# Nucleus search of step 2: three rounds that aim 6.5 values short, in place of four that aim 8 short

## The chip, the cores and the metric

The kernel runs on one core of a Trainium2 chip. The metric is the device time of one execution in microseconds (us), as a median of several runs. Engines are named as in the profile: PE (TensorE matmul), PEld (TensorE weight load), DVE (VectorE), ACT (ScalarE), POOL (GpSimd), SP (SyncE, here mostly the issuer of loads).

## The reference, cut to what matters

There are 2708 nodes with 512 features. Layer 0 is a graph attention layer. Layer 1 makes two steps (s = 0, 1; this document calls them step 1 and step 2, as the change does). Each step builds an attention matrix over all node pairs, keeps of each row only the nucleus (the largest values, until they hold 90% of the row's mass), and multiplies:

```python
def _adj_from_feats(Xa, W1, W2, W3):
    logits = (Xa @ W1) @ W2 @ (Xa @ W3).T
    idx = jnp.argsort(-logits, axis=1)
    vals = jnp.take_along_axis(logits, idx, axis=1)
    csum = jnp.cumsum(jax.nn.softmax(vals, axis=1), axis=1)
    k_i = jnp.sum(csum < 0.9, axis=1) + 1          # how many of each row are kept
    ...
    return jax.nn.softmax(masked, axis=1)          # the others are -inf

for s in range(2):
    A = _adj_from_feats(Xa, W1, W2, W3)
    Xf = Rf @ Xf
    Xb = Rb @ Xb
    Xa = A @ Xa
    Z = Z + (Xf @ U1[s] + Xb @ U2[s] + Xa @ U3[s])
Y = X + Z                                          # then a layer norm, and the residual
```

Rf and Rb are the row- and column-normalised adjacency.

## The kernel before, in words

**Tiles.** The 2708 rows are 22 tiles of 128 (the last has 20 rows). Attention works on pairs of tiles: 11 pairs, numbered 0 to 10. For one pair the work goes through these stages:

- `queries` loads the pair's queries, `products` (PE, line 570) makes the logits of both tiles against all 2708 keys, and ACT copies them to two SBUF tiles `p` (line 572). There are four buffers `p`, so two pairs' worth.
- the row maximum (`maxima`, DVE, line 597), then `exp`: ACT turns `p` into exponentials, POOL works out three first guesses of the threshold, ACT looks at the mass above each (`junk_a`, line 604, twelve passes over 2708 columns), and POOL adds these looks up (`masses`, line 629, tile `pts`).
- `Opened.ready` (line 691) and `bracket` (from line 697): DVE takes from the three looks the two points of each row that lie on either side of the wanted mass.
- `search`: in each round `point` (lines 718 to 726, nine tiny DVE instructions) picks a threshold between the two ends, `measure` (line 683, one DVE pass over 2708 columns for each tile of the pair, with an accumulator) finds the mass above it, and five tiny instructions (lines 768 to 773) move one of the ends. `AIM` says by how many values the search aims to stop short of the wanted mass, so that it ends just above the nucleus' last value. `ROUNDS` is the number of rounds in step 1 and step 2.
- `finish`: for each tile, the `NEXT` largest values below the threshold are taken, eight at a time (a masked copy into `keep[0]`, line 877, then MAX8, line 879). Among these the last value of the nucleus is found; `kept_ranked` (lines 817 to 820) writes the kept exponentials to `keep`, ordering equal values by `rank`. `NEXT` is 16 in step 2 before and after.
- `branch`: a code is loaded from SBUF and DVE branches on it (line 961). If a row of the pair did not find its last value among the 16, `short` sets the code and `bisect` runs for the pair: 27 halvings with two passes each, then two scans of each tile. If only the number of equal values does not come out, `ties` runs for a tile (lines 826 to 836, with a scan over 2708 columns, line 831).
- the reciprocal of the kept mass (`rden`, line 972) ends the pair's search. `attended` then transposes `keep` on PE (line 1146), ACT copies the transposes (line 1150), and PE multiplies them with the values (line 1168). There are two buffers `keep`, one pair's worth.

**Order.** The schedule of PE, ACT, DVE and SP is written out by hand. The loop over g runs from -1 to 10. In iteration g, PE first makes `products` of pair g + 2, then `attended` of pair g. Between its pieces are put, as `others`, the products with the adjacency matrix (line 1042, operands `hl` of 512 KB and `s_r` of 256 or 192 KB loaded by SP for every one, in 3 and 4 buffers) and with U1 and U2 (line 1062), shared out evenly over the pairs by `price`; and as `fills` the ACT steps of `exp` of pair g + 2. What is left of both comes in a loop at the iteration's end. Meanwhile DVE runs `search` of pair g + 1. In its rounds are put: before the second measurement and after the second round the two maxima of pair g + 2 (`early`'s first two functions); before the third measurement the layer norm statistics of the rows finished one iteration ago (line 153); and before the fourth measurement the rest of that norm (lines 1242 and 1243, tile `yo`). SP stores these rows (line 1244) at one fixed place of its in-order queue, in the middle of `attended`; loads that come later in the program wait behind that store.

The search's rounds read:

```python
        for it in range(ROUNDS[s]):
            o.point(s > 0 and it == 0)
            if it == 1:
                afterwards.extend(early())
            if afterwards:
                afterwards.pop(0)()
            o.measure()
            ...
            if it == 1:
                afterwards.pop(0)()
        for rest in afterwards:
            rest()
```

Of the kernel before, what the change touches and what calls it, by code (L numbers as in the profile page):

```python
# [42 lines left out]

CURVE = 0.4
CAP = 0.06
AIM = (4.0, 8.0)
ROUNDS = (2, 4)
NEXT = (8, 16)

TINY = 2.0 ** -80  # L50
# [4 lines left out]
def kernel(  # L55
# [591 lines left out]
    class Opened:  # L647
# [27 lines left out]
        def aim(self, dst, th):  # L675
            v, lg = nc.vector, self.lg
            v.scalar_tensor_tensor(dst, th, AIM[lg.s], lg.cap, op0=OP.mult, op1=OP.min)
            v.scalar_tensor_tensor(dst, lg.tot, 1.0 - P_NUC + CURVE, dst, op0=OP.mult, op1=OP.add)
# [58 lines left out]
    def search(lg, o, junk, early, late):  # L737
# [22 lines left out]
        afterwards = []  # L760
        for it in range(ROUNDS[s]):
            o.point(s > 0 and it == 0)
# [723 lines left out]
```

## Time and profile before

| what | us |
|---|---|
| median of 3 runs (3461.5 to 3477.28) | 3462.85 |
| the profiled execution's own time | 3462.71 |
| its span, first to last instruction | 3460.9 |
| PE busy | 3183.6 (92%) |
| DVE busy | 2573.5 (74%) |
| ACT busy | 1502.3 (43%) |
| POOL busy | 933.6 (27%) |

Times inside the profile are counted from the span's start. Step 1's pairs run from about 1000 to 2050, the first search of step 2 ends at 2292.9, its other ten searches end at 2396.7, 2513.9, 2634.6, 2740.8, 2844.1, 2951.4, 3073.8, 3180.1, 3302.1 and 3401.9 (line 972), and the rest is the last pair's product and norm. An "x" in a row counts instructions; "idle before" is the time that the engine stood still ahead of them, with what ended most of it. A PE that is shown busy need not be at its peak, since the ends of matmuls are modelled.

### The profile page before, as it was taken

To read this page: it belongs to the slowest core of one execution; us is meant where nothing else is said; L and a number is where in the kernel's file an instruction comes from. 1 tells how busy PE (TensorE), PEld (TensorE's weight loads), DVE (VectorE), ACT (ScalarE), POOL (GpSimd) and SP (SyncE) were. 2 spreads that over 40 slices of the span, in tenths; PEclk is the share of its full clock that TensorE was granted. 3 is DMA by queue.
4 is the path that set the end of the run, shared out by engine and by line. 5 is a ranking of instruction groups with operands and counts; after the bars stand their busy time and mean duration, and the time that the engine had idled before them with its cause. 6 is when DMAs were issued, how large, how long until landed. Compare 5 with 4: busy or idle time off the path is not lost. (4 is left out here: it accounts for less than half of the span.)

```text
span 3460.9 us, 44356 instructions
## 1 busy us (share of the span) xinstructions
PE 3183.6 (92%) x16033; PEld 1695.6 (49%) x16033; DVE 2573.5 (74%) x4485; ACT 1502.3 (43%) x2219; POOL 933.6 (27%) x1091
## 2 busy tenths in 40 slices
PE   7988899998888999999999998899988999998998
PEld 4543333332455446455564643555555555555553
DVE  4588899899857564463745634997999899898893
ACT  2333231111046766665657622346544564455510
POOL 4221743607221222122122312111321233122211
PEclk9998999999999999999999999999999999999999
DMA  4478554222386245254453534865544653556553
GB/s 135 153 240 271 188 176 146 85 93 87 114 291 222 92 143 206 67 187 165 140 181 122 199 124 141 281 220 189 188 137 139 207 200 125 175 182 220 182 178 123
DMA packets 240046, 580.65 MB, mean 168 GB/s; under 512 B 32863, under 2 KB 66107, under 8 KB 239657
## 3 DMA queue, kind: packets, MB, share of 16 engines
q1 hardware_dynamic: 217721, 503.38, 43.9%
q0 software_dynamic: 22064, 74.09, 5.6%
q8 instruction: 127, 2.08, 0.2%
q14 instruction: 134, 1.10, 0.1%
HBM read 471.68 MB, written 105.68 MB: 167 GB/s over the span
## 5 line engine op out<-in xcount | busy, mean ns | idle before, releaser
L1168 PE MATMUL a<-va,at 128*128 128x512 f32 (+2 forms) x1936 | 887.2, 598 | 4.7 <-ACT at L1150 4.6
L483 PE MATMUL po<-e,fw 128*32 128x384 f32 (+3 forms) x7392 | 675.7, 502 | 65.7 <-DVE e L477 38.7
L477 DVE SCALAR_TENSOR_TENSOR e<-r_b,kk,a_c 128x768 f32<-128x768 f32 (+3 forms) x704 | 659.7, 997 | 50.4 <-PE po L483 41.8
L604 ACT ACTIVATE junk_a<-p,nth 128x2708 uint8<-128x2708 f32 (+1 forms) x240 | 612.7, 2553 | 38.1 <-POOL nth L619 33.6
L1042 PE MATMUL q<-hl,s_r 128*128 128x512 f32 x1936 | 541.5, 426 | 70.8 <-DMA s_r<-s_d 49.8
L1168 PEld LDWEIGHTS a<-va,at 128*128 128x128 f32 (+2 forms) x1936 | 338.2, 186 | 373.8 <-issue 341.4
L1042 PEld LDWEIGHTS q<-hl,s_r 128*128 128x128 f32 x1936 | 365.1, 193 | 235.5 <-issue 67.2
L483 PEld LDWEIGHTS po<-e,fw 128*32 128x32 f32 (+1 forms) x7392 | 256.9, 112 | 449.7 <-issue 260.0
L1150 ACT COPY at<-t 128x512 f32<-128x512 f32 (+3 forms) x308 | 140.9, 478 | 652.4 <-PE t L1146 648.6
L683 DVE SCALAR_TENSOR_TENSOR junk<-p,th 128x2708 bf16<-128x2708 f32 (+1 forms) x132 | 407.3, 3086 | 3.0
L1062 PE MATMUL q<-u_k,v 128*128 128x512 f32 x704 | 316.9, 592 | 1.1 <-ACT v L1052 1.1
L1045 PE MATMUL q<-s_r,hl 128*128 128x512 f32 (+1 forms) x1056 | 279.7, 409 | 17.7 <-DMA s_r<-s_d 15.1
L1045 PEld LDWEIGHTS q<-s_r,hl 128*128 128x128 f32 x1056 | 193.2, 189 | 97.7 <-issue 49.9
L1062 PEld LDWEIGHTS q<-u_k,v 128*128 128x128 f32 x704 | 133.3, 190 | 158.9 <-issue 154.2
L570 PE MATMUL t<-keys,q_t 128*128 128x452 f32 x528 | 158.7, 424 | 52.4 <-ACT p L572 50.6
L572 ACT COPY p<-t 128x452 f32<-128x452 f32 (+2 forms) x264 | 131.5, 537 | 172.0 <-PE t L570 128.0
L879 DVE MAX8 vn<-keep 128x8 f32<-128x2708 f32 (+1 forms) x66 | 196.8, 2981 | 2.3
L597 DVE TENSOR_REDUCE nmx<-p 128x1 f32<-128x2708 f32 (+1 forms) x44 | 130.5, 2967 | 63.9 <-ACT p L572 63.9
L1215 PE MATMUL a<-u_k,v_t 128*128 128x512 f32 (+1 forms) x352 | 170.2, 624 | 4.7 <-ACT yo L1222 3.0
L155 POOL TENSOR_SCALAR ln_rs<-ln_mv 128x1 f32<-128x1 f32 x66 | 49.6, 752 | 412.8 <-DVE ln_mv L154 411.5
L1146 PEld LDWEIGHTS t<-ident,keep 128*128 128x128 f32 (+1 forms) x968 | 115.5, 139 | 77.5 <-issue 48.0
L1146 PE MATMUL t<-ident,keep 128*128 128x128 f32 (+1 forms) x968 | 146.0, 273 | 3.5 <-ACT p L572 2.8
(311 smaller groups left out, 3435.3 us busy)
## 6 DMA issues: line engine op xcount, KB each, us to landing
hl<-vhl_d SPq DMA_DIRECT2D x132, 512.0 KB
s_r<-s_d SPq DMA_DIRECT2D x264, 256.0 KB
hl<-fhl_d SPq DMA_DIRECT2D x132, 512.0 KB
hl<-bhl_d SPq DMA_DIRECT2D x132, 512.0 KB
u_k<-in_L_gnn_U_dram SPq DMA_DIRECT2D x184, 256.0 KB
arow<-in_adj_dram SPq DMA_DIRECT2D x42, 677.0 KB
s_d<-a_f SPq DMA_DIRECT2D x66, 384.0 KB
s_r<-s_d SPq DMA_DIRECT2D x132, 192.0 KB
```

The lines of the kernel that those rows point to most:

```text
L477: nc.vector.scalar_tensor_tensor(es[i][:pr, :cw], r_b[:pr, i, :cw], kk[:pr, t, grp[i]:grp[i] + 1], a_c[t][:pr, :cw], op0=OP.max, op1=OP.mult)
L483: nc.tensor.matmul(po[k][n][q * w:(q + 1) * w, :b - a], lhsT=of if d < DH else of.to_broadcast([pr, w]), rhs=es[i][:pr, a:b], start=(t == ...
L570: nc.tensor.matmul(pl[:, :c1 - c0], lhsT=q[:, i], rhs=self.keys[:, c0:c1], start=(i == 0), stop=(i == 1))
L604: nc.scalar.activation(junk[:pr], self.p[i][:pr], func, **kw)
L683: nc.vector.scalar_tensor_tensor(self.junk_b[:pr], p, th, p, op0=OP.is_ge, op1=OP.mult, accum_out=dst)
L879: v.max(vs, keep[0][:pr])
L1042: nc.tensor.matmul(half[j], lhsT=s_r[:, j * P:(j + 1) * P], rhs=hl[:, h], start=(c == 0 and h == 0), stop=(c == NT - 1 and h == 1))
L1045: nc.tensor.matmul(half[j][:, :w], lhsT=hl[:, h, j * P:(j + 1) * P], rhs=s_r[:, :w], start=(c == 0 and h == 0), stop=(c == NT - 1 and h == 1))
L1062: nc.tensor.matmul(half[j], lhsT=across_t[-1][k][:, j * P:(j + 1) * P], rhs=u_k, start=(start and k == 0), stop=(start and k == KD - 1))
L1146: nc.tensor.transpose(pt[:rows[c], j, :pr], keep[i][:pr, cols[c]], ident[:pr, :pr])
L1168: nc.tensor.matmul(pa[:pr], lhsT=at[:rows[c], j, :pr], rhs=va[:rows[c], c, :], start=(c == 0), stop=(c == NT - 1))
L1215: nc.tensor.matmul(pz[i][:rows[t]], lhsT=v_t[i][:, k, :rows[t]], rhs=u_k, start=(k == 0), stop=(k == KD - 1))
```

## The change

Two constants change. `AIM` and `ROUNDS` hold a value for step 1 and one for step 2; those of step 1 and `NEXT` stay. In step 2 every pair's search makes three rounds, and aims 6.5 values short of the wanted mass. The rest of the norm (lines 1242 and 1243) then follows the third round instead of standing between the fourth round's `point` and its measurement. On PE, ACT, POOL and SP the instructions and their order are the same, but for the place of the empty block joins of line 961 among them.

```diff
 CURVE = 0.4
 CAP = 0.06
-AIM = (4.0, 8.0)
-ROUNDS = (2, 4)
+AIM = (4.0, 6.5)
+ROUNDS = (2, 3)
 NEXT = (8, 16)
```

## The prediction

> **What bounds the kernel now.** First the page's busy shares: PE 92%, DVE 74% over the whole span. That is an average, so next the windows view, cut at the ends of step 2's searches (line 972). Columns: length, then busy us of PE, PEld, DVE, ACT, POOL, then the granted PE clock, DMA share, GB/s.
>
> ```profile
> 2513.80:2634.50 120.70, 106.67 (x360) 64.18 (x360) 111.34 (x189) 61.45 (x72) 26.32 (x22) 0.95 0.49 164
> 2740.70:2844.10 103.40, 95.85 (x321) 56.96 (x322) 94.25 (x180) 58.02 (x66) 29.53 (x22) 0.97 0.46 157
> 2951.40:3073.80 122.40, 112.23 (x372) 65.55 (x371) 110.60 (x189) 58.86 (x68) 26.39 (x24) 0.97 0.55 183
> 3180.10:3302.10 122.00, 111.55 (x373) 63.88 (x374) 108.52 (x189) 56.95 (x65) 22.39 (x21) 1.00 0.62 212
> ```
>
> A pair of step 2 takes 100 to 122 us, and both DVE and PE stand still for only some 10 us of it. DVE's 10 us are its own chain, not waits: some 5 us of it follow the branch of line 961 in nearly every pair. So two engines are close to full, and the question is which one sets the pace where. The waits of PE between 2292 and 3402 answer it; they come to about 90 us.
>
> ```profile
> L1042 PE MATMUL q<-hl,s_r 128*128 128x512 f32 x1584 | 449.8, 430 | 56.7 <-DMA s_r<-s_d 36.1 <-ACT xe L1086 20.0
> L570 PE MATMUL t<-keys,q_t 128*128 128x452 f32 x216 | 68.0, 443 | 29.0 <-ACT p L572 29.0
> ```
>
> PE waits mostly for loads and for ACT, hardly for DVE by name. But line 572 writes the buffers `p` that DVE's `finish` reads, so I looked in the timeline at what ACT waited for each time PE stood still at line 570, and at the one long load wait:
>
> ```profile
> 2405.65 6.58 PE L570 MATMUL t<-keys,q_t 128*128 128x452 f32 x17 [4.87 <-ACT p L572]
> 2513.88 0.97 ACT L572 COPY p<-t 128x452 f32<-128x452 f32 x2 [14.96 <-DVEq L961]
> 2514.47 7.51 PE L570 MATMUL t<-keys,q_t 128*128 128x452 f32 x20 [5.30 <-ACT p L572]
> 2634.67 0.97 ACT L572 COPY p<-t 128x452 f32<-128x452 f32 x2 [9.36 <-DVE keep L836]
> 2635.26 3.62 PE L570 MATMUL t<-keys,q_t 128*128 128x452 f32 x8 [9.22 <-ACT p L572]
> 2740.81 0.97 ACT L572 COPY p<-t 128x452 f32<-128x452 f32 x2 [17.51 <-DVEq L961]
> 2741.39 1.11 PE L570 MATMUL t<-keys,q_t 128*128 128x452 f32 x4 [2.07 <-ACT p L572]
> 3302.04 1.06 PE L1146 MATMUL t<-ident,keep 128*128 128x128 f32 x8 [0.62 <-DVEq L966]
> 3342.37 1.84 SPq L1244 DMA_DIRECT2D out_dram<-yo  x2
> 3348.66 5.46 PE L1042 MATMUL q<-hl,s_r 128*128 128x512 f32 x12 [5.23 <-DMA s_r<-s_d]
> ```
>
> At 2513.9, 2634.7 and 2740.8 ACT's copy was let go by the end of DVE's search: there DVE is the bound. At 2405 it was not: ACT itself came straight from the looks of line 604, and DVE too stood still 9.2 us for their sums (line 691 on POOL's line 629). After 2844 PE never again waits for `p`. It is late there: its first transpose starts 8 to 21 us after the search has ended (2844 to 3200). At 3342 SP had been waiting for DVE's norm before it could issue more loads, and PE waited for those.
>
> **What the change removes.** One round per pair, 11 in all. From the groups on DVE: `point` 203+187+166+175+188+167+161+168+164 = 1579 ns; two passes of 3086 ns and two accumulator reads of 82 ns = 6336 ns; the five after it 297+166+227+210+244 = 1144 ns. Together 9.06 us; the timeline has two rounds starting 8.94 us apart (2324.42, 2333.36). I take 9.0, so 99 us of DVE work leave the kernel, all of it in step 2. Nothing is added on DVE. The norm's second half moves ahead by the removed `point`, 1.6 us. No DMA, PE, ACT or POOL instruction goes; the pacing of `others` and `fills` does not depend on the rounds.
>
> **What of it reaches the end.** Only where PE waits for DVE, so I follow PE's delay pair by pair.
>
> - First search (ends 2292.9): PE's wait just after it, 2.29 us at 2299, is ACT's backlog of copies (xe), and DVE's next search cannot start before its looks at about 2285. Nothing gained.
> - Search ending 2396.7: DVE would be 9 us or more earlier, and wait for the looks, which end at 2405.9 as now. Nothing gained.
> - Search ending 2513.9: it starts at 2406 as now and ends 9.0 earlier, at 2505. PE came to its wait at 2509.2: all 5.30 us go.
> - Search ending 2634.6 (with `ties`, hence 121 us): starts 9.0 earlier, just after its looks (2504.6), and ends at 2616.6. PE, 5.3 earlier, wants the buffer at 2619 to 2620: the 9.22 us go.
> - Search ending 2740.8: the 2.07 us go as well. From here PE leads by 16.6 us and DVE by more, and what is late next is PE: DVE will wait for the looks, which ACT makes at the end of PE's iteration.
> - Searches ending 2844 to 3302: no PE wait for DVE is left to remove except 0.62 us at 3302.
> - 3342: the norm comes some 20 us earlier against PE's own work, since DVE now starts ahead of PE; the loads follow in time: 5.23 us go.
>
> Sum of waits: 5.30 + 9.22 + 2.07 + 0.62 + 5.23 = 22.4 us. Behind two of them PE also runs slowly: after 3348.66 twelve matmuls of line 1042 take 5.46 us where the same twelve at 3357.63 take 3.33; after 2635.26 eight of line 570 take 3.62 us, against 17 in 6.58 at 2405, which is 3.1 for eight. The granted clock is 0.51 from 2630.5 to 2640.7 and 0.52 from 3347.3 to 3354.1. I add 3 us. [...]
>
> So 22.4 + 3 = 25.4 us. The span falls from 3460.9 to 3435.5; the profiled execution's own time of 3462.71, which lies 1.8 over the span and within 0.2 of the median, falls to **3437**. Of 99 us of DVE work about three quarters turn into DVE standing still.
>
> **Terms that the trace does not show.** Two new waits on DVE. (1) `keep[0]` is overwritten by line 877 some 51 us after a search's start, now 42; PE's transposes of that tile end 24 to 47 us after the previous search's end. DVE will wait up to 8 us in the pairs where PE is latest (3180). Behind it on DVE are only its own finish and branch, 53 to 70 us; PE wants the result some 75 us after these transposes. Cost to PE: between 0 and 8 us, taken as 0. (2) The maxima (line 597) may wait for `products` up to 5 us; the same slack covers them. Of PE's other 64 us of waits (36.1 and 20.0 in line 1042, 7.2 at 2299 and 2405) the change could shrink some or add to them, since everything shifts: bounds half of them gone (some 27 us more gain), or the three `p` waits, 16.6, coming back. I take 0.
>
> **Rivals.**
>
> 1. *DVE sets the pace everywhere*: 9 to 11 rounds of 9.0 reach the end, 3363 to 3381, say 3370. For it: DVE's idle time is its own chain. Against: PE has just 90 us of idle time there, 56 of it for loads and for xe, which DVE does not make, and after 2844 PE is the late one. [...]
> 2. *The loads take the place of DVE*: PE's stop at line 570 lets the three `hl` and four `s_r` buffers fill; without it PE meets line 1042 sooner and waits for `s_r`. Then the 16.6 us and their slow clock come back: 3437 + 18 = 3455. For it: 36 us of such waits, most after 2940 where PE does not stop at line 570. Against: `products` themselves run 7 to 8 us without any load of lines 1035 and 1037 being used up.
> 3. *Slower: three rounds do not bring some row within 16 values, and its pair runs `bisect`.* Price, never in this trace (line 683 has 132 + 12 passes, just the rounds'): 27 times two passes of 3.12 us and some 0.6 of small ones, 185 us, then about eight passes of 3 us for each of two tiles, 48 us: 230 us for a pair, 3437 + 230 = 3670 for one. It decides from one single row that needs a 17th value. I followed the search row by row in ordinary arithmetic on the reference's inputs: with four rounds and aim 8 the worst row needs 16 of the 16, with three and 6.5 the worst needs 15, with three and 8 two rows would need 17. Shifting the logits at random by 1e-4 does not change it; by 1e-3 one or two rows can fall out. So the aim is what keeps the change safe here, with a margin of one value.
>
> That the change does not do what it says is not open: only the rounds and their aim are in the program's difference, which is 11 rounds on DVE.
>
> **Chances.** Forecast 0.70, rival 1 0.06, rival 2 0.17, rival 3 0.07. What this measurement tells from no change is about 0.5%, 17 us, so faster means below 3445.5. The forecast's size is uncertain by the 8 us of new waits above and half of the 64 us below; a few of its cases end inside 0.5%. Faster 0.70 - 0.05 + 0.06 = 0.71; same 0.17 + 0.05 = 0.22; slower 0.07. The range leaves out rivals 1 and 3: from 3410 (27 us more gain) to 3455 (rival 2).
>
> **What would show it.** Right: line 683's group th falls to x110, DVE's busy time to about 2475; the waits of 5.3, 9.2 and 2.1 us at line 570 are gone; DVE waits for POOL's line 629 at line 691 in most pairs after the third, and at line 877 for line 1146 in some; PE's idle time from the first search's end to the last falls from 90 to about 67 us. Wrong: pairs of 92 to 94 us (rival 1), more `s_r` waits with DVE idle (rival 2), a pair of over 300 us with over 50 more passes of line 683 (rival 3).

## The result, and the profile after

The changed kernel takes 3434.86 us (median of 8 runs, 3431.51 to 3456.8) against 3463.48 (8 runs, 3461.34 to 3477.28): 28.6 us less, a ratio of 0.9921 with a 95% interval of 0.9895 to 0.9946. The forecast was 3437.

The profiled execution of the changed kernel took 3456.8 us with a span of 3455.0, at the upper end of its runs, and the reason lies ahead of everything that the change touches. In the waits of ACT between 550 and 620 us (layer 0), 27.0 us go to one load of the adjacency, and 2.4 to 4.1 to each of six others; the kernel before has no such row there.

```profile
ACT a_c L454 <- DMA a_f<-in_adj_t_dram: 47.3, 7, 27.0
```

The columns are us in total, times, longest. So step 2's first search ends at 2315.3 in this execution, 22.4 us later than in the one of before (2292.9), although nothing up to then but that search has changed. I therefore compare from that point on: to the end it was 1168.0 us before and is 1139.7 after, 28.3 less.

That point is DVE's, and PE stands elsewhere in its own work there: it begins its next `products` 2.8 us after the search's end before (at 2295.7), and 14.8 us after it in the changed kernel (at 2330.1). Counted on PE, from its first `products` of step 2 to the end, both executions hold the same 4016 matmuls (length, busy us of PE, clock, DMA share, GB/s; before, then after):

```profile
2145.60:3460.90 1315.30, 1198.06 (x4016) 0.97 0.55 183
```

```profile
2177.00:3455.00 1278.00, 1186.09 (x4016) 0.98 0.56 189
```

This stretch is 37.3 us shorter: PE stands still 25.3 us less (117.2 to 91.9), and is busy 12.0 us less with the same matmuls. One pair of executions thus gives 28 or 37 us, by where the count begins, and the change is measured by the medians' 28.6.

The windows of the same four searches as in the prediction (length; busy us of PE, PEld, DVE, ACT, POOL; clock; DMA):

```profile
2537.20:2633.20 96.00, 94.58 (x329) 56.44 (x328) 86.28 (x162) 57.61 (x66) 23.19 (x19) 1.00 0.54 183
2727.80:2835.90 108.10, 100.25 (x335) 58.68 (x336) 86.44 (x162) 52.16 (x62) 25.79 (x21) 0.97 0.50 167
2945.80:3072.10 126.30, 114.36 (x387) 67.35 (x386) 100.23 (x170) 67.75 (x75) 28.56 (x25) 0.99 0.57 187
3168.40:3294.20 125.80, 112.64 (x378) 65.54 (x379) 101.09 (x171) 60.59 (x69) 35.77 (x26) 0.99 0.61 207
```

DVE is busy 7 to 10 us less in the second to fourth of them and 25 in the first, but of these four only the first is shorter. (Of the six that are not shown, the fourth, eighth and tenth of the ten are shorter too, by 9 to 12 us.) In the other three shown DVE stands still for 22 to 26 us where it was 9 to 14: they are now as long as PE makes them. All ten searches together take 1069.2 us, 1109.0 before. The end gains less than these 39.8 us, because the last search's result now waits for PE: PE's first transpose of it (line 1146) starts 16 us after the search's end, where it was 5. In all eleven pairs this start lies 11 to 33 us behind the end of the search, 0 to 21 before. What DVE waits for between the first and the last search, before and after:

```profile
DVE rden L972 <- DVEq L961: 41.0, 8, 6.3
DVE pts L691 <- POOL pts L629: 11.0, 3, 9.2
...
DVE nmx L597 <- ACT p L572: 1.0, 1, 1.0
```

```profile
DVE pts L691 <- POOL pts L629: 52.0, 7, 22.1
DVE rden L972 <- DVEq L961: 42.3, 9, 5.6
DVE nmx L597 <- ACT p L572: 18.3, 4, 10.3
DVE keep L820 <- PE t L1146: 12.8, 4, 6.3
DVE keep L877 <- PE t L1146: 12.0, 6, 5.9
```

The branch (line 961) costs what it did. The other rows of the second list are waits for the looks, for `products` and for PE's transposes, that is, for work that PE sets the pace of. And the same two groups of PE, between the same points:

```profile
L1042 PE MATMUL q<-hl,s_r 128*128 128x512 f32 x1584 | 441.8, 425 | 43.7 <-DMA s_r<-s_d 30.2 <-ACT xe L1086 12.8
...
L570 PE MATMUL t<-keys,q_t 128*128 128x452 f32 x216 | 63.3, 419 | 14.5 <-ACT p L572 14.5
```

Line 570's idle time fell from 29.0 to 14.5 us, line 1042's from 56.7 to 43.7, and all of PE's in the ten searches from 89.2 to 62.2. Over the same 4016 matmuls as above, the waits of line 570 for `p` fell from 29.7 to 15.5 us, those of line 1042 for `xe` from 20.0 to 12.8 and for `s_r` from 49.8 to 45.8.

### The profile page after: what moved, and what is told of

The parts are those of the page before. It is cut to its first block, busy times and chain, and to the rows that moved or that the text cites. A ratio compares the mean times of both kernels' runs of the same rounds, so it can differ in the third digit from the quotient of the medians.

```text
span 3455.0 us, 44145 instructions
## 1 busy us (share of the span) xinstructions
PE 3182.8 (92%) x16033; PEld 1707.9 (49%) x16033; DVE 2455.9 (71%) x4278; ACT 1498.9 (43%) x2219; POOL 934.5 (27%) x1091
## 5 line engine op out<-in xcount | busy, mean ns | idle before, releaser
L1042 PE MATMUL q<-hl,s_r 128*128 128x512 f32 x1936 | 536.2, 424 | 59.4 <-DMA s_r<-s_d 45.8
L483 PEld LDWEIGHTS po<-e,fw 128*32 128x32 f32 (+1 forms) x7392 | 270.1, 112 | 459.8 <-issue 216.7
L683 DVE SCALAR_TENSOR_TENSOR junk<-p,th 128x2708 bf16<-128x2708 f32 x110 | 339.8, 3089 | 2.5
L570 PE MATMUL t<-keys,q_t 128*128 128x452 f32 x528 | 156.7, 422 | 40.9 <-ACT p L572 37.3
L454 ACT ACTIVATE a_c<-a_f 128x768 bf16<-128x768 f32 (+1 forms) x88 | 67.3, 765 | 190.9 <-DVE e L477 102.6
```

The costliest lines, as they stand in the source:

```text
L483: nc.tensor.matmul(po[k][n][q * w:(q + 1) * w, :b - a], lhsT=of if d < DH else of.to_broadcast([pr, w]), rhs=es[i][:pr, a:b], start=(t == ...
L570: nc.tensor.matmul(pl[:, :c1 - c0], lhsT=q[:, i], rhs=self.keys[:, c0:c1], start=(i == 0), stop=(i == 1))
L683: nc.vector.scalar_tensor_tensor(self.junk_b[:pr], p, th, p, op0=OP.is_ge, op1=OP.mult, accum_out=dst)
L1042: nc.tensor.matmul(half[j], lhsT=s_r[:, j * P:(j + 1) * P], rhs=hl[:, h], start=(c == 0 and h == 0), stop=(c == NT - 1 and h == 1))
```

## The experiments

The theory: up to about 2741 DVE sets step 2's pace and after that PE does, so of 99 us of DVE work only PE's waits for DVE come out at the end. The rival: DVE sets the pace, and something else (loads, the ties branch, the aim) explains why the gain is small. Ratios are to the kernel before, run on the same chip.

### More and fewer rounds

Five, four and two rounds, all with the aim of 6.5:

```diff
-ROUNDS = (2, 3)
+ROUNDS = (2, 4)        # or (2, 5), or (2, 2)
```

In the kernel with two rounds, `short` and `over` are set to zero too, so the branch is never taken and rows that are not found keep too few values.

> Four rounds in step 2 as before, with the new aim of 6.5. My theory: the aim itself costs no time, only the round does, so this is the kernel before: 3458 to 3468 us, line 683 x132. It also tells whether the ties branch of the search that ends at 2634.6 before (17 us on DVE, gone in the changed kernel: line 831 x2 in place of x3) went with the aim or with the round: x3 here says with the round, x2 with the aim. If it went with the aim and those 17 us of DVE matter, this kernel loses PE's wait of 9.2 us at that place and comes out near 3450. Rival: the aim carries the gain by itself; then 3435.

> Five rounds, aim 6.5: one more than before, two more than after. My theory: DVE then sets the pace of all ten pairs, so the tenth of a round that PE hides at three rounds is gone: 10 x 9.0 us over four rounds, less the 11 us that DVE waits for the looks in the kernel before: 3535 to 3555 us, some 85 us for the fifth round against 28 us for the fourth. Rival (each round is worth the same at the end, as if DVE and PE shared a common slow-down): 3462 + 28 = 3490 us.

> Two rounds, aim 6.5; the flags that choose bisect and ties in step 2 are set to zero, so rows that are not found among 16 values keep too few, and no pair takes a branch. This leaves out part of the computation. DVE has 99 us less than after, and two ties branches of 17 us less. My theory: PE sets the pace already at three rounds, so nearly nothing comes of it: 3425 to 3437 us, and DVE waits the rest (line 691 for the looks, line 877 for the transposes). Rival (DVE still sets the pace after the change): 3435 - 90 = 3345 us.

| rounds (aim 6.5) | us | ratio, 95% interval |
|---|---|---|
| 5 | 3519.90 | 1.0161, 1.0127 to 1.0194 |
| 4 | 3472.76 | 1.0028, 1.0004 to 1.0051 |
| 3 (the change) | 3434.86 | 0.9921, 0.9895 to 0.9946 |
| 2, no branches | 3429.63 | 0.9909, 0.9875 to 0.9944 |

The steps are worth 47, 38 and 5 us, from one and the same 99 us of DVE work. (The intervals of the last two rows overlap: the 5 us are not told from nothing. The kernel with two rounds also lacks the two ties branches.) The third round less is nearly free of effect, as the theory said, and DVE's waits in the kernel with two rounds say where it went (its lines from 915 on stand one higher):

```profile
DVE keep L877 <- PE t L1147: 100.5, 9, 18.7
DVE pts L691 <- POOL pts L629: 89.0, 10, 21.5
```

Two expectations missed. Four rounds with the new aim are 5 to 15 us slower than I expected, and five rounds 15 us faster than the lowest that I expected. As far as the traces show, both come from the ties branch, which I had counted as given. It runs three times with aim 8 (searches ending 2634.6, 3073.8 and 3302.1 before), three times with four rounds and aim 6.5 but in the eighth, ninth and tenth pair, and twice with five rounds. In the kernel with four rounds three such branches stand one after the other at the end, and PE waits for the last:

```profile
3310.56 1.73 PE L1146 MATMUL t<-ident,keep 128*128 128x128 f32 x7 [12.47 <-DVEq L966]
```

My test in the expectation, x3 against x2, was a bad one: the count stayed at three, the places moved. In the fourth pair the branch is gone with aim 6.5 (three, four and five rounds) and there with aim 8 (three and four rounds), so it goes with the aim. In the groups of the kernel with five rounds PE waits at line 570 for 66 us, and DVE has no wait for the looks (line 691) left: DVE is the pace of every pair there.

```profile
L1042 PE MATMUL q<-hl,s_r 128*128 128x512 f32 x1584 | 444.7, 426 | 58.7 <-DMA s_r<-s_d 32.3 <-ACT xe L1086 25.9
L570 PE MATMUL t<-keys,q_t 128*128 128x452 f32 x212 | 75.2, 490 | 66.4 <-ACT p L572 65.7
```

### Three rounds with the old aim

```diff
-AIM = (4.0, 6.5)
+AIM = (4.0, 8.0)
```

> Three rounds with the old aim of 8. Followed row by row in ordinary arithmetic, two rows (in the first and the eighth of the eleven pairs) need a 17th value, so both pairs should run bisect: line 683 x110 + 108 = x218, and some 230 us more on DVE for each. My theory: time 3435 + 2 x 230 less what PE has in hand, 3850 to 3900 us. Rival: the aim makes no difference to which rows are found; then 3435 us and line 683 x110.

3853.38 us, ratio 1.1127 (1.1082 to 1.1172). Both pairs ran `bisect`: line 683 in the groups of DVE, and PE at the two places in the timeline:

```profile
L683 DVE SCALAR_TENSOR_TENSOR junk<-p,th 128x2708 bf16<-128x2708 f32 x218 | 670.1, 3074 | 6.3
```

```profile
2503.65 5.25 PE L570 MATMUL t<-keys,q_t 128*128 128x452 f32 x12 [206.35 <-ACT p L572]
```

A second wait, of 195.8 us, stands at 3462. So the rival of a slower kernel was real, with its price (some 209 us at the end for each pair, against 230 on DVE), and the aim of 6.5 is what keeps the change out of it. That two rows among 2708 decide rests on the row-by-row arithmetic; the trace shows that the two pairs it named ran `bisect`.

### PE made lighter, with and without the change

In both kernels step 2 leaves out its products with U1 and U2, and their loads:

```diff
                 def through(u, k, start):
+                    if last:
+                        return
```

> Four rounds as before, but step 2 leaves out the products with U1 and U2 of line 1062 and their loads (352 matmuls of 429 ns start to start, 151 us of PE); part of the computation is left out. My theory: DVE has no less to do and already sets the pace of step 2's first pairs, so the time falls by much less than 151 us: 3415 to 3445 us. Rival (PE sets the pace of step 2 already before): 3465 - 130 = 3335 us.

> Three rounds, with the same products and loads left out. My theory: with PE out of the way the round is worth what it takes on DVE, 9.0 us in each of ten or eleven pairs, less what the looks on ACT now hold back: 70 to 99 us under the four-round kernel without these products, so some 3330 to 3365 us. Rival (loads or ACT's looks, not PE, take over the pace after the change): the two light kernels lie only some 28 us apart, as the full ones do.

| us | four rounds, aim 8 | three rounds, aim 6.5 | difference |
|---|---|---|---|
| all of PE's work | 3463.48 | 3434.86 | 28.6 |
| without line 1062 in step 2 | 3449.65 | 3360.80 | 88.9 |
| difference | 13.8 | 74.1 | |

The time of the kernel before was 3463.54 us beside the light kernels, so the two lines can be compared. The ratios of the light kernels are 0.9968 (0.9955 to 0.9982) and 0.9706 (0.9688 to 0.9724). PE is busy 111 us less in the first of them (3183.6 to 3072.3 in the pages' first part), and 14 us come of it: with four rounds DVE sets the pace. At 3449.65 it lies 5 us above the range that I expected: even less of PE's work came out. PE's idle time at line 570, 29.0 us before, shows what it waited for instead:

```profile
L570 PE MATMUL t<-keys,q_t 128*128 128x452 f32 x212 | 78.3, 516 | 73.8 <-ACT p L572 73.5
```

With PE out of the way the same round is worth 89 us of its 99. In the changed kernel PE's work is worth 74. The two engines hide each other, and this is the plainest evidence for the theory. The products and their loads went together, so their shares are not separated; but PE's waits for the loads that are left, `s_r`, did not shrink with it (68.5 us with four rounds, 36.1 in the full kernel).

By the left column DVE is the engine to shorten in the kernel before. How far this goes stands in the last column: 29 of DVE's 99 us come out beside all of PE's work, 89 without line 1062.

### The ties branch, taken away and put back

```diff
                 v.tensor_scalar(over, over, 0.25, None, op0=OP.is_gt)
+                if grp == pairs[3]:
+                    v.memset(over, 0.0)             # in the kernel before
+                    v.memset(over[:, 1:2], 1.0)     # or this, in the changed kernel
```

> Four rounds and aim 8, but the ties branch of step 2's fourth pair is kept from running (its flag is set to zero; a few rows may keep an equal value too many). In the changed kernel this branch did not run either, which I had not foreseen. DVE has 17 us less in the search that ended at 2634.6. My theory: PE's waits of 9.2 and 2.1 us at line 570 go, and from there PE leads: 11 to 14 us less than before, 3450 to 3455 us. Rival (the branch lies beside other work): 3463 us.

> Three rounds and aim 6.5, and the ties branch is made to run for the second tile of step 2's fourth pair, as it did before the change: 17 us of DVE put back there. My theory: DVE then ends that search at 2650 against PE's need at 2646, so PE waits some 4 us and no more: 3435 to 3441 us; then the round removed the larger part of the wait of 9.2 us and the branch's absence only the last of it. Rival (the branch's absence, not the round, made that part of the gain): 9 to 12 us back, 3445 to 3448 us.

Without the branch the kernel before takes 3455.54 us, ratio 0.9973 (0.9955 to 0.9992), 8 us less, at the upper edge of the 3450 to 3455 that I expected; PE's idle time at line 570 falls to 18.1 us. The changed kernel with the branch put back takes 3433.61, ratio 0.9928 (0.9911 to 0.9945), the same as without it and a little under the 3435 to 3441 that I expected. Its timeline shows PE's wait at the place: 1.6 us, where I had reckoned with 4.

```profile
2600.12 5.80 DVE L831 TENSOR_TENSOR_SCAN p<-junk 128x2708 f32<-128x2708 bf16 x1
```

```profile
2612.89 3.51 PE L570 MATMUL t<-keys,q_t 128*128 128x452 f32 x8 [1.57 <-ACT p L572]
```

So either the round or the branch going is enough for that term, and since the round is there the branch adds nothing.

### The norm one round earlier, in the kernel before

```diff
             if afterwards:
                 afterwards.pop(0)()
+            if it == 2 and afterwards:
+                afterwards.pop(0)()
             o.measure()
```

> Four rounds and aim 8 as before, but the rest of the norm (lines 1242 and 1243) stands before the third measurement, beside the statistics, so DVE has the rows of tile yo ready some 8 us earlier in every pair and nothing else changes. My theory: SP's store of line 1244 lets the loads behind it go 8 us earlier, PE's load wait of 5.2 us (4.5 to 7 us in the kernels with four rounds) in the middle of the last search goes, and with it at most 5 us of the end, since PE then meets the last search: 3456 to 3462 us, in the trace no load wait over 2 us near 3345. Rival (those loads are late for a reason of their own): the wait stays, 3463 us.

3462.71 us, ratio 1.0013 (0.9993 to 1.0034): no difference, where I had expected 1 to 7 us. The load wait is gone, as its cause was the norm: SP's store starts at 3323.05 (3342.37 before), and in the middle of the last search no load wait is left. But in this kernel with four rounds DVE is as late as before, and PE, earlier, meets it twice (lines stand two higher):

```profile
3295.95 1.06 PE L1148 MATMUL t<-ident,keep 128*128 128x128 f32 x8 [2.51 <-DVEq L968]
```

```profile
3394.10 1.84 PE L1148 MATMUL t<-ident,keep 128*128 128x128 f32 x8 [2.29 <-DVEq L963]
```

### What PE's own waits are worth, with and without the change

First, in the changed kernel, the ACT steps of `exp` let in earlier in step 2's first iteration:

```diff
-att = attended(..., 1 if final else 3 if g else len(tgroups) + (1 if last else -1))
+att = attended(..., 1 if final else 3 if g or last else len(tgroups) - 1)
```

> The changed kernel; in step 2's first iteration the ACT steps of exp are let in from the third piece of attended on, as in the others, in place of the seventh. My theory: the looks for the next search then end earlier, PE's wait of 4.7 us for ACT at the start of the next iteration goes (in the changed kernel at 2440, DVE waits 22 us there for the looks), and nothing else stands between: 3427 to 3431 us. Rival (ACT's passes delay the copies of the transposes that PE needs, line 1150, by as much): 3433 to 3440 us.

3428.72 us, ratio 0.9901 (0.9881 to 0.9920), 6 us under the changed kernel in the medians though the intervals overlap; PE's wait of 4.7 us for ACT is not in its trace. Then more loads under way, in both kernels:

```diff
-sp = tile_pool(name=f"s{s}sp", bufs=4 if last else 3, ...)
+sp = tile_pool(name=f"s{s}sp", bufs=3, ...)                       # s_r
-hl = sp.tile([P, 2, D], F32R, name="hl", bufs=3)
+hl = sp.tile([P, 2, D], F32R, name="hl", bufs=4 if last else 3)
-u_k = up.tile([P, D], F32, name="u_k", bufs=3)
+u_k = up.tile([P, D], F32, name="u_k", bufs=2 if last else 3)
```

> The changed kernel with four hl buffers of 512 KB in step 2 in place of three; to make room s_r has three in place of four and u_k two in place of three. PE waits some 46 us for these loads in step 2. My theory: PE now sets the pace, so each wait that goes reaches the end; if they come from too few loads under way, 10 to 25 us go: 3410 to 3425 us. Rival (the loads are limited by what the DMA engines move, or by s_r): 3433 to 3445 us.

> Four rounds and aim 8 as before, with the buffers of the last experiment (four hl, three s_r, two u_k), which took 34 us off the changed kernel. My theory: with four rounds DVE has only some 11 us of waits in step 2's searches, so PE's faster loads can give no more than about that: 3450 to 3458 us, and PE's waits at line 570 grow. Rival (the loads' gain does not depend on the round): 34 us as well, 3429 us.

The changed kernel falls to 3399.88 us, ratio 0.9820 (0.9797 to 0.9842), the fastest complete kernel of this study and 10 us below the range that I expected. The kernel before with the same buffers stays where it was: 3461.64, ratio 0.9986 (0.9959 to 1.0013), though its profiled execution took 3481.32. PE's groups, with the change and without it:

```profile
L1042 PE MATMUL q<-hl,s_r 128*128 128x512 f32 x1589 | 437.9, 423 | 29.6 <-DMA s_r<-s_d 15.4 <-ACT xe L1086 13.7
L570 PE MATMUL t<-keys,q_t 128*128 128x452 f32 x216 | 64.4, 424 | 14.8 <-ACT p L572 14.8
```

```profile
L1042 PE MATMUL q<-hl,s_r 128*128 128x512 f32 x1623 | 455.2, 428 | 39.6 <-ACT xe L1086 20.5 <-DMA s_r<-s_d 18.1
L570 PE MATMUL t<-keys,q_t 128*128 128x452 f32 x216 | 69.7, 454 | 32.9 <-ACT p L572 32.5
```

The load waits were halved in both (30.2 to 15.4 with the change; 36.1 to 18.1 without). Only where DVE had been taken off the pace did that reach the end; without the change line 570's wait grew, and one of 12.7 us for the ties branch appeared. I had allowed the kernel before 5 to 13 us. The 35 us of the changed kernel are more than these waits: over the same 4016 matmuls of step 2, PE stands still 21.9 us less than in the changed kernel (91.9 to 70.0) and is busy 8.5 us less. The 5 us beyond that are not explained.

## Why the prediction was right

- **What sets the pace**: right: DVE before and PE after the change, as the light kernels and the kernel with two rounds show. That in the kernel before DVE has the pace up to 2741 and PE from there is read from the waits, and was not tried pair by pair.
- **99 us of DVE work leave**: line 683 went from x132 to x110, DVE's busy time from 2573.5 to 2455.9, 117.6 less. Of the 18.6 over my sum some 14 are one ties branch (14.1 us of DVE from 2620.5 on in the kernel before, behind a wait of 4.5; the expectations have 17), which I had not foreseen, and it does not reach the end (put back, it changed nothing). The rest are the same instructions taking less time, line 818 for one (71.5 to 68.6 us).
- **Nothing gained at the first two searches**: right. PE's waits of 2.29 us (now at 2333) and 4.66 (at 2440, 4.87 before) are still there; they are ACT's.
- **5.30, 9.22, 2.07 and 0.62 us**: all gone. Line 570's idle time fell by 14.5 us against 16.6; some smaller waits there grew.
- **5.23 us behind the norm**: gone, and for the reason given. SP waits less for the norm in these ten searches (before, then after), and no load wait over 1 us is left in the middle of the last search. That the change gained these 5 us at its end was not tried by itself: in the kernel before, the earlier norm gave nothing.

```profile
SPq L1244 <- DVE yo L1243: 88.7, 16, 22.5
```

```profile
SPq L1244 <- DVE yo L1243: 19.5, 6, 6.7
```

- **The two new waits on DVE**: there, at lines 877 and 597, and a third that I had not named, at line 820 (12.8 us, the second tile's transposes). None reaches PE: the kernel with two rounds has 100 us of the first kind and is no slower.
- **PE's other waits, taken as unchanged**: those for ACT's copies `xe` fell by 7.2 us (20.0 to 12.8), a term that I had set to 0. It goes with the rounds: from 2270 on these waits are 16.5 to 24.7 us in the five kernels with four rounds and all of PE's work, and 12.8 to 15.2 in the five with three or two. How a round reaches them was not followed. My 64 us of other waits also held the 5.23 that I had already counted. The waits for `s_r` fell by 4.0 over the same matmuls, where 5.23 were forecast; so rival 2, loads in DVE's place, did not happen. They are all the same what PE waits for most after the change, and the buffers' 35 us lie there.
- **Idle time of PE** from 90 to 67: 89.2 to 62.2, and 25.3 us less over the same 4016 matmuls, where the sum has 22.4.
- **Slow clock behind the waits, 3 us**: too small. PE is busy 12.0 us less with the same 4016 matmuls. The granted clock of this stretch rose from 0.97 to 0.98 (a hundredth of its 1300 us, an estimate, is 13), that of the fourth search from 0.95 to 1.00. With four rounds and all of PE's work, five kernels are busy 1195.0 to 1198.6 us here, and four with three or two rounds and the old buffers 1185.5 to 1190.7, so the term is 4 to 13 us if the clock is all of the difference. I had added it behind two waits, but a slow stretch stands behind shorter ones too, in the kernel before after the 2.07 us at 2741 (length, busy us of PE, clock, DMA share, GB/s):

```profile
2743.20:2746.60 3.40, 3.40 (x9) 0.53 0.01 2
```

- **The sum**: 25.4 us stand against 28.6 in the medians, but against 37.3 in the one pair of profiles that shows its terms. The waits for DVE and for the norm's loads were right to some 3 us; the nearness of the forecast, 2 us, is in part luck, for the slow clock and the `xe` waits were put too low by more than that.
- **Rivals**: 1 is out by the kernel with two rounds; 3 is what three rounds with the old aim do.

Left open: why fewer rounds shorten the `xe` waits, and the spread of some 25 us between executions of one kernel, which hides terms of a few us.

## What to carry to other kernels

Where two engines are both near full, count what the other one waits for, not what the shortened one loses: the gain ends where the next engine takes over, here after 29 of 99 us. A change that then gives nothing may have been hidden the same way: the loads' extra buffer was worth nothing before this change and 35 us after it. And where a fast path falls back on a slow one for a single row, follow the data through it before its time is believed.

## What the runs showed that was not expected

ACT waited 27.0 us for one load of layer 0 in one execution, in a part that no kernel here changes; runs of one kernel spread over some 25 us, so the profiles were compared from a point inside, and the choice of that point alone moved the difference between 28 and 37 us. And the ties branch moved from pair to pair with the search's aim and rounds, some 14 us of DVE each; as far as the traces show, this is why the kernels with four and five rounds missed the times that I expected by 5 to 15 us.
